# Dealing out a generator's pieces anew: layer 2's early keys and values in a four-layer kernel on one core

## The chip, the cores and the metric

The kernel runs as one program on one core of one Trainium2 chip. The metric is the device time of one execution in microseconds, less is better. Before the change it is 2393.62 us, the median of three runs (2391.97 to 2395.31). One more execution, taken with the hardware profiler, is the one that the rows in this document come from.

## The reference: what is computed

A stack of four layers works on tokens x of shape (4, 256, 256) and on a context of shape (4, 1601, 256), all float32. Each layer is a cross step followed by a feed-forward network, both added to x:

- Layer 0: softmax attention of the tokens over the masked context, then a mixture of 32 experts (96 inner channels), of which each token takes 8.
- Layer 1: a summary of the context by a decayed scan, added through layer norms, then 8 experts with 2 for each token and a shared expert.
- Layer 2: attention with 16 heads of 128 channels and 4 key/value heads, over the 1601 keys and values of the context and causally over the 256 tokens of the batch. Keys are normed (root mean square). Then 4 experts, 1 for each token.
- Layer 3: attention with 32 heads of 8 channels over the context, then a feed-forward network with quantised weights.

What matters for this change is one part of layer 2. Its context keys and values depend on the context and on weights alone, not on x:

```
k_ctx = rms_norm(ctx @ wk_ctx) * k_norm_w      # per batch and key/value head: 1601 x 128
v_ctx = ctx @ wv_ctx                            # per batch and key/value head: 1601 x 128
```

So they can be made at any time before layer 2's first scores.

## The kernel before

The kernel is written as a sequence of stages, layer by layer. The order of instructions on each engine is mostly that of the program text, rearranged by a scheduler in the framework where instructions are not pinned; semaphores are derived from the tiles' uses.

**The early pieces.** `l2_early` (from L1263) is a generator that makes the context keys and values of layer 2 for 16 units (4 batches by 4 key/value heads). It yields after each of 176 pieces, 11 for a unit:

- Seven product pieces. Six hold four matmuls (L1307) from `ctxT` and the unit's weights into one tile of the accumulator memory, 128 rows each for two chunks of the context. The last holds two matmuls with 96 rows. A matmul appears as two records in the profile. ScalarE (ACT) copies the keys to `kr_early` (L1314) and the values to `va_early` (L1315), and the SP queue writes the values to DRAM (L1316, `vd`). After some pieces ACT squares the keys into `sq_early`, a tile with one buffer (L1325), and VectorE (DVE) sums them (L1326).
- The norm of the unit: a square root on ACT and a reciprocal on DVE (L125, L126), and four multiplications (L1332) by the engine in `self.scaler`. That is GpSimd (POOL), but DVE inside `l0_add` and at the end of `l1_ffn`.
- Four turn pieces, for the unit before: 4, 4, 4 and 1 transposes (L1341), each piece copied by ACT into `kT_early` (L1343, 4 buffers) and written by SP (L1344, `kd`).

**Where pieces are advanced.** `self.fill(n)` (L174) advances the generator by n pieces; what it issues stands in the program at that place. The counts are constants at the top of the file:

- three pieces at the start of layer 0's attention;
- `F0[4]` = 6 behind layer 0's router logits, `F0[5]` = 8 within `slots`, which counts the tokens of each expert, `F0[6]` = 4 at each of four parts of the matmuls that build `src`, the list of tokens sorted by expert (L512), and `F0[7]` = 4 after the gathers by `src` are issued on POOL (L522);
- `G0` = 9 at each of nine steps of `l0_add`, which gathers the experts' results and adds them to x, 81 in all;
- `F1` = 1, 2, 2, 3 in `normed` (L187) ahead of layer 1's FFN, one count for each batch, between the layer norm `xn` (L160) and its transposes `tp_ln` (L191);
- `G1`, 30 in sum, at the end of layer 1's FFN, between the adds of its results to x (L981);
- `LN2` = 2, `Q2` = 2 and `C2` = 6 in layer 2's first `prep`, behind the norm of the first batch (transposes `tp_ln`, L1425), and behind the first queries;
- what is left is drained ahead of the first scores:

```
            for n, _ in enumerate(prep(0, w, ready)):
                self.fill(Q2 if n == 0 else C2 if n == 3 else 0)
            for _ in self.early:
                pass
            self.es2.close()
```

Before the change ten pieces are left for this drain (the three last products of unit 15, the turns of units 14 and 15 in part). `prep` makes the tokens' own queries and keys of a unit: `tpq` (projection of the queries), `tpkv` (keys and values), the steps `qo` and `ko` on DVE and POOL (L1482 to L1516), the transposes `tpqT` (L1526) and `tpk` (L1531). Then the scores `s` start.

**Layer 0's expert loop.** In `l0_ffn` the sorted tokens form 95 tiles. `brought(n)` transposes a gathered tile `f0xr` (L561, `f0tpx`), `through(n)` does the first matmuls (`f0gu`), `turned(n)` transposes the inner values (`f0tph`), `down(n)` does the second ones (`f0y`). `brought` runs two tiles ahead:

```
            brought(0)
            brought(1)
            for s in range(NS + 2):
                if s < NS:
                    hs[s] = through(s)
```

Within this loop there are no early pieces.

Of the kernel before, what the change touches and what calls it, by code (L numbers as in the profile page):

```python
# [44 lines left out]
CT2 = NM - 1  # L45


F0 = [0, 0, 0, 0, 6, 8, 4, 4]
G0 = 9
REGS = 4  # L50
F1 = [1, 2, 2, 3]
G1 = [7, 4, 4, 3, 2, 2, 2, 2, 2, 2, 0]
LN2, Q2, C2 = 2, 2, 6
FIRST3 = [7, 1, 3]
# [43 lines left out]
class Kernel:  # L98
# [311 lines left out]
    def l0_ffn(self, one):  # L410
# [17 lines left out]
        with ExitStack() as es:  # L428
# [21 lines left out]
            nc.gpsimd.tensor_scalar(start, tok[:, 0:1], float(P), None, ALU.mult)  # L450
            xT = self.normed(ps, F0[:B], xd)
            next(loads)
# [4 lines left out]
            for t in range(8):  # L457
                for k in range(2):
                    self.mm(lg[:, t, :], xT[t // 4][:, k, (t % 4) * P : (t % 4 + 1) * P], wr[:, k, :], k == 0, k == 1)
            self.fill(F0[B])  # L460
            next(loads)
# [10 lines left out]
            nc.vector.tensor_single_scalar(oh, oh, GONE, ALU.is_equal)  # L472
            cum, end = self.slots(rt, "f0", E0, oh, products(), low, keep, lambda: self.fill(F0[B + 1]))
            next(loads)
# [18 lines left out]
            for part in range(4):  # L493
                ones = []
                for t in range(2 * part, 2 * part + 2):
# [9 lines left out]
                    ones.append((t, rows, cols))  # L505
                self.fill(F0[B + 2])
                next(loads, None)
# [26 lines left out]
            nc.vector.tensor_copy(ei, er[:1, :NS])  # L534
            self.fill(F0[B + 3])

# [21 lines left out]
            def brought(n):  # L558
                tp = ps.tile([P, 2, P], F32, name="f0tpx", tag="tp")
                for k in range(2):  # L560
                    nc.tensor.transpose(tp[:, k, :], xr[n][:, k * P : (k + 1) * P], self.ident)  # L561
                t = two.tile([P, 2, P], F32, name="f0xsT", bufs=4)
                nc.scalar.copy(t, tp)
                xsT.append(t)
                if n % REGS == 0:
                    expert.extend(self.registers(ei[:, n : min(n + REGS, NS)], E0))

            def through(n):
                gu = products()[:, : 2 * I0]
                for k in range(2):  # L570
                    self.mm(gu, xsT[n][:, k, :], w13[:, bass.ds(expert[n], 1), k, :], k == 0, k == 1)
                h = two.tile([P, I0], F32, name="f0h", bufs=3)
                nc.scalar.activation(h, gu[:, :I0], AF.Silu)
                nc.vector.tensor_tensor(h, h, gu[:, I0:], ALU.mult)
                return h

            def turned(h):
                tp = ps.tile([P, P], F32, name="f0tph", tag="tpf")
                nc.tensor.transpose(tp[:I0], h, self.ident)
                hT = two.tile([I0, P], F32, name="f0hT", bufs=3)  # L580
                nc.scalar.copy(hT, tp[:I0])
                return hT

            def down(n, hT):
                y = ps_y.tile([P, 512], F32, name="f0y", tag="y")[:, :D]
                self.mm(y, hT, w2[:, bass.ds(expert[n], 1), :], True, True)
                ys = two.tile([P, D], F32, name="f0ys", bufs=6)
                nc.vector.tensor_copy(ys, y)
                nc.sync.dma_start(yd[n * P : (n + 1) * P, :], ys)

            hs, hTs = {}, {}
            brought(0)
            brought(1)
            for s in range(NS + 2):
                if s < NS:
                    hs[s] = through(s)
                    if s + 2 < NS:
                        brought(s + 2)
                if 0 <= s - 1 < NS:
                    hTs[s - 1] = turned(hs.pop(s - 1))  # L600
                if s >= 2:
                    down(s - 2, hTs.pop(s - 2))
                if s >= 20 and s % 4 == 0:
                    next(gated, None)
# [166 lines left out]
    def l1_ffn(self, weights):  # L771
# [11 lines left out]
        with ExitStack() as es:  # L783
# [14 lines left out]
            low, keep, lane, tok = self.low, self.keep[:, :E1], self.lane, self.tok  # L798
            xT = self.normed(ps, F1[:B], xd, rt)

# [1687 lines left out]
```

## Time and profile before

| | us |
|---|---|
| median of three runs | 2393.62 |
| profiled execution, device time | 2387.69 |
| its span, first to last instruction | 2386.0 |
| around the span | 1.69 |
| TensorE (PE) busy | 2255.6 |
| DVE busy | 1473.2 |
| ACT busy | 1272.4 |
| POOL busy | 948.7 |

The mean granted clock of PE is 0.973 of full speed. Where rows of the profile are shown, a timeline row has the start in the span, the duration, the engine, the line, the operation with its tiles, the count, and in brackets the idle time before it with what released it. A row of a window has its limits and length, then the busy time of PE, of weight loads, DVE, ACT and POOL with the number of instructions, then PE's clock, the share of the DMA engines and their rate in GB/s. A row of waits has the total, the times and the longest.

### The profile page before, as it was taken

How to read it: one execution, taken by the hardware profiler on the slowest of the kernel's cores; microseconds unless marked ns; L12 is line 12 of the kernel's file. 1: busy time of each engine (PE TensorE's matmuls, PEld its weight loads, DVE VectorE, ACT ScalarE, POOL GpSimd, SP SyncE). 2: the span in 40 equal slices, each digit the busy share in tenths (PEclk: the TensorE clock that was granted, in tenths of full speed). 3: DMA queues.
4: the chain of work that ended last, by engine and by line, in shares of the span. 5: the costliest groups of instructions: out<-in, count | busy, mean ns of one | idle time of the engine just before them, and what ended most of it. 6: DMA issues, size and time to landing. Idle time of an engine off the chain costs nothing.

```text
span 2386.0 us, 42230 instructions
## 1 busy us (share of the span) xinstructions
PE 2255.6 (95%) x14335; PEld 1382.2 (58%) x14335; DVE 1473.2 (62%) x3553; ACT 1272.4 (53%) x2877; POOL 948.7 (40%) x1707
## 2 busy tenths in 40 slices
PE   8989997889989999999999999999899889999996
PEld 5677875777745555555555655555665533444332
DVE  5453532773457777777777777777334574758344
ACT  3334443552474555555555555553232577888994
POOL 1014655503335544555554555554121253334220
PEclk9989998989999999999999999999899999999998
DMA  7165575652550111111111111100534353434320
GB/s 267 41 201 161 172 156 157 197 185 65 167 179 32 43 51 47 47 51 51 51 52 51 51 51 50 44 10 10 205 124 117 114 156 103 109 94 103 83 64 19
DMA packets 156078, 234.47 MB, mean 98 GB/s; under 512 B 33929, under 2 KB 122761, under 8 KB 154666
## 3 DMA queue, kind: packets, MB, share of 16 engines
q1 hardware_dynamic: 138998, 190.07, 25.0%
q0 software_dynamic: 11280, 31.60, 5.4%
q10 hardware_dynamic: 5588, 10.09, 1.4%
q8 instruction: 117, 1.92, 0.3%
q14 instruction: 95, 0.78, 0.1%
HBM read 169.94 MB, written 61.74 MB: 97 GB/s over the span
## 4 chain that ended last, share of the span: by engine, by line
PE 78%; DVE 7%; issue 5%; DMA 4%; ACT 2%; POOL 2%; SPq 1%; ACTq 0%; POOLq 0%; DVEq 0%
PE o L117 17%; PE s L117 17%; PE o L77 6%; PE b L77 3%; PE f2gu L117 3%; PE s L77 3%; PE f1gu L117 2%; PE fill L1307 2%; PE f0gu L117 2%; PE acc L117 2%; PE tpq L117 2%; PE av L117 2%; PE f0y L117 2%; PE f2y L117 1%; PE f1y L117 1%
## 5 line engine op out<-in xcount | busy, mean ns | idle before, releaser
L1572 ACT ACTIVATE p<-s,nmsm 128x448 f32<-128x448 f32 (+2 forms) x512 | 324.7, 639 | 369.6 <-DVE nmsm L1567 317.4
L117 PE MATMUL o<-pT,va 128*128 128x256 f32 (+2 forms) x1920 | 431.7, 377 | 3.3 <-DVE pT L1613 2.9
L117 PE MATMUL s<-kT,qT 128*32 128x448 f32 (+2 forms) x4096 | 424.2, 550 | 4.2 <-ACT p L1572 4.2
L77 ACT ACTIVATE e<-s 128x1024 f32<-128x1024 f32 (+1 forms) x416 | 392.4, 1041 | 57.4 <-PE s L77 56.3
L117 PEld LDWEIGHTS o<-pT,va 128*128 128x128 f32 (+1 forms) x1920 | 344.7, 190 | 127.9 <-issue 75.4
L1607 POOL TENSOR_SCALAR p<-p,rm 128x448 f32<-128x448 f32 (+2 forms) x512 | 320.7, 649 | 6.3
L1567 DVE TENSOR_REDUCE nmsm<-s 128x1 f32<-128x448 f32 (+4 forms) x384 | 293.2, 783 | 4.4
L1613 DVE STREAM_TRANSPOSE pT<-p 128x448 f32<-128x448 f32 (+4 forms) x384 | 278.1, 778 | 11.1 <-POOL p L1607 11.1
L117 PEld LDWEIGHTS s<-kT,qT 128*32 128x32 f32 x4096 | 121.7, 109 | 250.2 <-issue 213.9
L77 PE MATMUL o<-e,va 128*32 128x512 f32 x1656 | 246.9, 614 | 12.3 <-DVE os L77 12.2
L1600 POOL TENSOR_TENSOR rm<-em,tot 32x8 f32<-32x8 f32 x256 | 50.3, 197 | 335.6 <-DVE tot L1597 303.3
L1564 DVE TENSOR_TENSOR s<-s,mask 128x64 f32<-128x64 f32 (+4 forms) x384 | 92.5, 260 | 128.5 <-PE s L117 82.4
L77 PEld LDWEIGHTS s<-qb,kb 32*128 32x128 f32 (+1 forms) x1664 | 65.5, 180 | 182.3 <-issue 143.7
L1307 PE MATMUL fill<-wkc_early,ctxT 128*128 128x256 f32 (+1 forms) x444 | 110.5, 401 | 8.9 <-ACT va_early L1315 6.7
L522 POOL DMA_INDIRECT f0xr<-f0xd,f0src x95 | 91.3, 961 | 66.5 <-PE f0y L117 25.5
L77 PE MATMUL s<-qb,kb 32*128 32x256 f32 (+1 forms) x1664 | 111.5, 331 | 3.1 <-ACT e L77 1.8
L77 POOL CAST kb<-kf 128x384 fp32r<-128x384 f32 (+1 forms) x126 | 65.5, 549 | 96.4 <-PE s L77 61.8
L1307 PEld LDWEIGHTS fill<-wkc_early,ctxT 128*128 128x128 f32 (+1 forms) x444 | 87.0, 200 | 25.3 <-ACT va_early L1315 7.8
L1572 ACT ACTIVATION_READ_ACCUMULATOR p<-s,nmsm 128x1 f32 x512 | 100.5, 196 | 0.0
L1326 DVE TENSOR_REDUCE ss_early<-sq_early 128x4 f32<-128x512 f32 x64 | 37.1, 580 | 82.8 <-ACT sq_early L1325 72.0
L630 POOL DMA_INDIRECT f0yt<-f0yd,f0slot x64 | 63.1, 987 | 60.7 <-DVE x L622 29.8
L117 PE MATMUL f2gu<-f2wgu,f2xsT 128*128 x176 | 85.1, 608 | 0.6 <-ACT f2xsT L114 0.3
(579 smaller groups left out, 3689.2 us busy)
## 6 DMA issues: line engine op xcount, KB each, us to landing
kf<-kd SPq DMA_DIRECT2D x384, 48.0 KB
vd<-va_early SPq DMA_DIRECT2D x96, 128.0 KB
kd<-kT_early SPq DMA_DIRECT2D x48, 256.0 KB
kT<-kd SPq DMA_DIRECT2D x16, 768.0 KB
va<-vd SPq DMA_DIRECT2D x16, 768.0 KB
kd<-kt SPq DMA_DIRECT2D x96, 128.0 KB
f0yd<-f0ys SPq DMA_DIRECT2D x95, 128.0 KB
ctxT<-in_ctxT SPq DMA_DIRECT2D x5, 1664.0 KB
```

The costliest lines, as they stand in the source:

```text
L77: ins = f(*a, **kw)
L117: self.ordered(self.nc.tensor.matmul(out, lhsT, rhs, start=start, stop=stop, **kw))
L522: nc.gpsimd.indirect_dma_start(out=t, out_offset=None, in_=xd[:, :], in_offset=bass.IndirectOffsetOnAxis(ap=src[:, n : n + 1], axis=0),)
L630: nc.gpsimd.indirect_dma_start(out=yt, out_offset=None, in_=yd[:, :], in_offset=bass.IndirectOffsetOnAxis(ap=slot[:, t, r : r + 1], axis=0),)
L1307: ins = nc.tensor.matmul(tp[:rows, t, :], ctxT[u // NKV2][:, k, c0 : c0 + rows], w[u % NKV2][:, k, :], start=k == 0, stop=k == 1,)
L1326: nc.vector.tensor_reduce(ss[:, m0:m1], sq[:, : m1 - m0, :], AX.X, ALU.add)
L1564: nc.vector.tensor_tensor(sv, sv, mask[:, e0:e1, : nt - CT, :].rearrange("p n t i -> p n (t i)"), ALU.add)
L1567: nc.vector.tensor_reduce(ms[:, 0, e0:e1], s[:, n0:n1, : nt * 32], AX.X, ALU.max, negate=True)
L1572: nc.scalar.activation(p[:, n, : nt * 32], s[:, n, : nt * 32], AF.Exp, bias=ms[:, 0, e : e + 1], accum_out=ms[:, 1, e : e + 1],)
L1600: nc.gpsimd.tensor_tensor(r[32 * a : 32 * a + 32], e[:, a], tot, ALU.mult)
L1607: nc.gpsimd.tensor_scalar(p[:, n, : nt * 32], p[:, n, : nt * 32], r[:, e : e + 1], 1.0, ALU.mult, ALU.mult)
L1613: self.pin(nc.vector.transpose(pT[:, 2 * c + n0 : 2 * c + n1, :nt, :].rearrange("p n t i -> p n (t i)"), p[:, n0:n1, : nt * 32],))
```

## The change

Four places get other counts. One piece more comes behind layer 0's router logits; one piece each is advanced between `brought(0)` and `brought(1)` and after the first `through`; one piece more comes in the first batch of `normed` ahead of layer 1's FFN. Since the pieces come in a fixed order, every later place advances other pieces than before: `l0_add` those numbered 40 to 120 (before: 37 to 117), the end of layer 1's FFN 130 to 159 (126 to 155), layer 2's `prep` 160 to 169 (156 to 165). The drain ahead of the scores is left with six pieces in place of ten.

```diff
-F0 = [0, 0, 0, 0, 6, 8, 4, 4]
+F0 = [0, 0, 0, 0, 7, 8, 4, 4]
 G0 = 9
 REGS = 4
-F1 = [1, 2, 2, 3]
+F1 = [2, 2, 2, 3]
...
             brought(0)
+            self.fill(1)
             brought(1)
             for s in range(NS + 2):
                 if s < NS:
                     hs[s] = through(s)
+                    if s == 0:
+                        self.fill(1)
                     if s + 2 < NS:
                         brought(s + 2)
```

## The prediction

> **What bounds the kernel now.** I read the page first: the busy line and the chain of waits.
>
> ```profile
> PE 2255.6 (95%) x14335; PEld 1382.2 (58%) x14335; DVE 1473.2 (62%) x3553; ACT 1272.4 (53%) x2877; POOL 948.7 (40%) x1707
> PE 78%; DVE 7%; issue 5%; DMA 4%; ACT 2%; POOL 2%; SPq 1%; ACTq 0%; POOLq 0%; DVEq 0%
> ```
>
> TensorE (PE) is busy for 95% of the span and carries 78% of the chain. The change adds and removes no matmul: it moves early pieces. So it can pay only where PE idles, or runs at a reduced clock, and a piece moved there no longer stands on PE elsewhere. The second view is therefore the table of windows, for the stages that the four edits touch (columns: PE, weight loads, DVE, ACT, POOL, then clock, DMA share, GB/s).
>
> ```profile
> 137.00:204.00 67.00, 60.94 (x270) 49.82 (x270) 33.45 (x107) 26.13 (x67) 10.95 (x13) 0.87 0.58 186
> 204.00:216.00 12.00, 7.54 (x39) 5.76 (x38) 1.79 (x6) 6.06 (x17) 8.83 (x9) 0.94 0.73 234
> 512.00:526.00 14.00, 13.22 (x47) 10.49 (x47) 4.61 (x18) 6.54 (x11) 3.40 (x4) 0.53 0.80 257
> 619.00:654.00 35.00, 33.89 (x172) 29.46 (x170) 19.03 (x52) 20.30 (x56) 14.41 (x15) 1.00 0.72 217
> 654.00:691.00 37.00, 28.85 (x127) 20.68 (x125) 18.42 (x49) 24.77 (x61) 15.47 (x19) 0.93 0.70 240
> 691.00:720.00 29.00, 24.78 (x186) 8.17 (x186) 21.79 (x50) 21.02 (x54) 10.94 (x25) 0.92 0.23 80
> ```
>
> Layer 0's routing (137 to 204) idles PE for 6 us of 67, its first gathers (204 to 216) for 4.5 of 12, layer 2's opening (654 to 691) for 8 of 37. Behind layer 1's first norm (512 to 526) PE is full but at clock 0.53. The end of layer 1's FFN (619 to 654) has only 1 us to spare. The waits of the gathers, of layer 1's norm, and of the opening, in three answers:
>
> ```profile
> PE f0tpx L561 <- DMA f0xr<-f0xd,f0src: 3.4, 2, 1.9
> PE f0gu L117 <- DMA vd<-va_early: 1.0, 1, 1.0
> ```
> ```profile
> 510.36 1.77 PE L191 MATMUL tp_ln<-ident,xn 128*128 128x128 f32 x8 [2.00 <-DVE xn L160]
> ```
> ```profile
> 653.59 0.60 PE L1425 MATMUL tp_ln<-ident,xn 128*128 128x128 f32 x4
> 658.87 2.02 PE L1307 MATMUL fill<-wkc_early,ctxT 128*96 128x256 f32 x4 [4.67 <-ACT va_early L1315]
> ...
> 671.87 1.89 PE L117 MATMUL tpkv<-wks,xT 128*128 128x256 f32 x8
> 673.60 5.34 PE L1307 MATMUL fill<-wkc_early,ctxT 128*128 128x256 f32 x24
> 679.89 0.66 PE L1526 MATMUL tpqT<-ident,qo 128*128 128x128 f32 x4 [0.96 <-POOL qo L1516]
> ...
> 683.94 1.98 PE L117 MATMUL tpq<-wq,xT 128*128 128x512 f32 x4
> 687.81 0.66 PE L1341 MATMUL fill<-ident,kr_early 128*128 128x128 f32 x4 [1.88 <-POOL kr_early L1332]
> 688.81 2.33 PE L1341 MATMUL fill<-ident,kr_early 128*128 128x128 f32 x9 [0.34 <-POOL kr_early L1332]
> 691.07 1.53 PE L117 MATMUL s<-kT,qT 128*32 128x416 f32 x8
> ```
> ```profile
> 684.69 1.28 ACT L125 ACT_TABLE_LOAD   x1
> ```
> ```profile
> 686.71 3.40 POOL L1332 TENSOR_TENSOR kr_early<-kr_early,ss_early 128x512 f32<-128x512 f32 x4 [5.88 <-DVE ss_early L126]
> ```
>
> This is the stage to read. The first unit's own keys and queries are turned by tpqT at 679.89 and by tpk, which ends at 683.2; the copy of tpk to kT ends at 683.9. The scores start 7.2 us later, because the rest of the early pieces is drained first: the last unit's norm waits for a table load, then POOL multiplies for 3.40 us, then come its transposes.
>
> **The change part by part**, against the profiled execution of 2387.69 us (span 2386.0 and 1.69 around it), which lies 5.93 below the median of the three runs, 2393.62. The median gets the same difference.
>
> *One piece more at layer 0's router (F0[4] 7 for 6).* In the instruction order, one product piece of four matmuls (eight records, 1.73 us at full clock in the chain's row, 2.0 at 0.87) stands on PE before the counts, and equally many matmuls stand before the first gather's transposes in both kernels. What can move is the gather list: later by 0 to 2.0. PE has gaps of 2.58, 1.21 and 1.80 us around the counts, so I take +0.6. Its ACT copies (two of 0.38) and its write on SP come earlier with it; ACT is busy for 26 of 67 us.
>
> *Two pieces among the first gathers.* They hold nine transposes with the one that shifts in (12 took 1.96 us, so 1.5), beside 4.5 us in which PE waits for DMA: nothing. Without that cover they cost 1.5. Three ACT copies of 0.69 stand ahead of the tile's own (ACT is busy for 6 of 12), and three writes of 256, 256 and 64 KB join gathers at a DMA share of 0.73. Bounds 0 to +1.5, taken 0.
>
> *One piece more at layer 1's first norm (F1[0] 2 for 1).* Up to tp_ln, PE gets four product matmuls more (+1.73), and four transposes between the later tp_ln go (-0.6). From 484 to 511 PE idles 5.3 us, 2.00 of them at the wait for xn, which DVE ends and PE's load doesn't touch: 0, with +1.7 as the upper bound. The lower bound is the half-clock stretch: if it follows from the idling, filling that saves up to 14 x (1 - 0.53) = 6.6 us.
>
> The Trainium skill ("TensorE: Matmul & The Clock Gate", HAM oscillation) puts the fall to half clock behind idle gaps of over about 3.4 us; by it, this piece would remove no slow stretch here, since the gap was 2.00.
>
> *End of layer 1's FFN.* PE's load there is equal (33.2 us against 33.3). The norm of unit 14 now falls on DVE (four multiplications in 2.08 and a reciprocal of 0.24) among the adds to x, for which layer 2's first norm waits; before, POOL did it at 663.17. DVE is busy for 19 of 35 us, so I take about half, +1.3: tp_ln ends at 655.5 and not 654.2. Bounds 0 to +2.3.
>
> *Layer 2's opening.* The stall of 4.67 us comes from ACT, whose copies queue behind squares with a single buffer, which DVE frees late, behind the adds. The stalled piece is now a transpose piece, and I take 1 us for the stall (0 to 5.3). From 656.5 PE's list up to tpkv is, start to start in the rows of before: a transpose 0.1, 12 products 5.2, tpq 1.72, 7 products 3.02, tpq 1.80, 7 products 3.0, tpkv 1.73: 16.6, so tpkv ends at 673.1. Before, it ended at 673.6. The first unit's chain after it (ko 0.97 and 0.73, qo 2.04 on POOL, tpqT, tpk, copies) is unchanged, but the last unit's norm now comes before it on POOL: ready some 1.7 us after the last product at 671.4, so POOL is held from 673.2 to 676.6, ko ends at 678.3 and qo at 680.4, where before qo ended at 680.84. So tpk's copy ends near 683.7 as before, and the scores start there and not at 691.07: -7.4. Left for later is unit 1's first tpq, which stood ahead of the scores. Bounds: a stall of 0 gives -8.4; one of 5.3 gives -3.1; POOL's 3.40 in full gives -4.0. The two other table loads fall after or out of this stretch; the one on the chain is worth 1.28 and is in the 7.4.
>
> The Trainium skill ("ScalarE: Activation LUTs", What ACT_TABLE_LOAD costs) puts a switch at 2.66 us with its drain. Here ACT's next instruction started 1.30 us after the load began, so the row goes; by the page I would have 1.4 us more for each load taken away.
>
> *Given back.* The moved tpq brings 1.98 us of PE, 0.59 of ACT, 2.05 of DVE and 1.27 of POOL into the first unit's scores, where DVE is busy for 21.8 of 29 us and PE idles 4.2: +1.2, bounds 0 to 2.05.
>
> Sum: 0.6 + 0 + 0 - 7.4 (the +1.3 is in it) + 1.2 = -5.6: 2382.1 for the profiled execution, 2388.0 for the median.
>
> **The rivals.** *A, the slow clock goes too.* The piece at layer 1's norm, or its other timing, ends the stretch at 0.53: 6.6 us, of which I count 6.0, so -11.6 and 2382.0. For it: the idle stands directly before the fall. Against it: 2.01 us of idle at 491.91 was followed by no fall.
>
> *B, the stall stays.* ACT's queue still blocks PE for 5.3 us in the opening: -3.1 + 0.6 + 1.2 = -1.3, so 2392.3. For it: the squares keep their one buffer. Against it: the transposes at the front use buffers that ACT empties earlier.
>
> *C, slower: the opening idles PE into half clock.* With 24 product records gone from behind tpkv, PE has 21 transposes (3.4 us) between 673.1 and tpqT at 680.4, so it idles for 4 us, where it idled 0.96. At layer 1's norm 2.00 us was enough for a stretch at 0.53. Price: 14 us of it cost 6.6, 20 us cost 9.4; with 9.4 and the gather list late by the full 2.0 (+1.4 on the 0.6) the sum is -5.6 + 9.4 + 1.4 = +5.2, so 2398.8. It decides if the granted clock is near 0.5 for over 12 us from 680 on. Against it: waits of 1.88 and 0.34 us just before 691 leave 691 to 720 at 0.92.
>
> By the page on the clock gate just named, an idle of 4 us in the opening is over the window, and this rule speaks against the change; one window of some 3.4 us at half clock would cost about 1.7 us, by estimate.
>
> **How the numbers follow.** The forecast has 0.48, its own range -8.5 to -3.0 (2385.1 to 2390.6); 0.2% or 4.8 us, about what a measurement of this kernel can tell, cuts off 0.09 of it as "same". A has 0.13, B 0.14, C 0.25. Faster: 0.39 + 0.13 = 0.52; same: 0.09 + 0.14 = 0.23; slower: 0.25. The range runs from A with a stall of 0 and the rest of the 6.6 (-13.2, 2380.4, rounded to 2380) to just above C's centre (2400), which leaves out some 0.15.
>
> **What would show it.** Right: scores that start about 7 us sooner after layer 2's tp_ln than 36.9 us, no wait on POOL's kr_early ahead of them, the first f0tpx less than 1 us later, equal spans from there to tp_ln of layer 1. Wrong: a gap of over 3 us for ACT's va_early or kT_early after layer 2's tp_ln (B); a clock near 0.5 behind 680 (C); a clock near 1 in the 14 us after layer 1's first tp_ln (A); or a loop of layer 0, untouched by the edits, that changes its length by more than 3 us.

## The result, and the profile after

The changed kernel takes 2400.31 us (median of 22 runs, 2395.95 to 2404.85), the kernel before 2394.76 (22 runs, 2389.08 to 2403.33). The ratio is 1.0023, 95% interval 1.0017 to 1.0030: 5.5 us slower, where 5.6 us faster was forecast.

The profiled execution took 2404.85 us, its span 2403.1. It lies 4.5 us above its median, and that of before 7.1 us below the median of the 22. So of the 17 us between the two profiles only a third is the change; a difference counts below only where other profiles repeat it. From the page of the changed kernel, busy line and chain:

```profile
PE 2266.2 (94%) x14322; PEld 1390.5 (58%) x14335; DVE 1476.9 (61%) x3557; ACT 1269.6 (53%) x2875; POOL 948.0 (39%) x1703
PE 79%; DVE 8%; issue 4%; POOL 3%; DMA 3%; ACT 2%; SPq 1%; ACTq 0%; POOLq 0%; DVEq 0%; another core or an unknown queue 0%
```

PE is busy for 10.6 us more with the same matmuls: they ran at a lower clock (0.967 in the mean, 0.973 before). DVE and POOL each have one hundredth more of the chain. The windows of the changed kernel, moved to where the stages now lie (layer 0's gathers, `l0_add`, behind layer 1's `tp_ln`, layer 2's opening), and ahead of them `l0_add` in the kernel before:

```profile
365.00:510.40 145.40, 116.29 (x539) 96.24 (x537) 88.23 (x217) 68.53 (x196) 63.15 (x64) 0.89 0.59 186
```
```profile
206.00:218.00 12.00, 7.16 (x31) 6.08 (x32) 1.43 (x5) 5.92 (x14) 9.23 (x10) 0.72 0.91 293
367.00:521.00 154.00, 121.72 (x548) 98.93 (x548) 90.50 (x219) 69.96 (x201) 67.85 (x68) 0.88 0.55 176
521.00:538.50 17.50, 16.62 (x54) 12.49 (x55) 6.34 (x22) 6.25 (x9) 0.00 (x0) 0.51 0.72 229
667.00:700.00 33.00, 26.54 (x109) 20.46 (x109) 16.30 (x41) 19.09 (x48) 9.73 (x12) 0.83 0.67 230
```

`l0_add` is 8.6 us longer, and the clock in the opening is 0.83 where it was 0.93. The waits at layer 1's norm and in the opening (timeline rows of PE, then one of POOL):

```profile
521.10 2.04 PE L191 MATMUL tp_ln<-ident,xn 128*128 128x128 f32 x8 [2.98 <-DVE xn L160]
...
666.99 0.78 PE L1428 MATMUL tp_ln<-ident,xn 128*128 128x128 f32 x4 [2.71 <-issue]
669.44 0.48 PE L1344 MATMUL fill<-ident,kr_early 128*128 128x128 f32 x1 [1.67 <-ACT kT_early L1346]
669.71 8.01 PE L1310 MATMUL fill<-wkc_early,ctxT 128*128 128x256 f32 x24
...
687.03 1.89 PE L117 MATMUL tpkv<-wks,xT 128*128 128x256 f32 x8
...
691.87 0.33 PE L1344 MATMUL fill<-ident,kr_early 128*128 128x128 f32 x1 [1.63 <-ACT kT_early L1346]
...
695.84 1.12 PE L1529 MATMUL tpqT<-ident,qo 128*128 128x128 f32 x4 [1.79 <-POOL qo L1519]
...
700.23 2.33 PE L117 MATMUL s<-kT,qT 128*32 128x416 f32 x11
```
```profile
689.75 3.55 POOL L1335 TENSOR_TENSOR kr_early<-kr_early,ss_early 128x512 f32<-128x512 f32 x4 [1.61 <-DVE ss_early L126]
```

The opening has the forecast order: transpose, 24 product records, tpq, 14, tpq, 14, tpkv, then POOL's norm ahead of ko and qo, and no wait on `kr_early` just ahead of the scores. But the 24 records took 8.01 us, not 5.2: the clock was halved from 668.3 to 675.1. Layer 1's `tp_ln` waits 2.98 us for DVE, where it waited 2.00.

Stage by stage, from the starts of timeline rows, one profile for each column. The last four columns are from the experiments, on other chips. In `l0_add` on the first chip, waits of PE that the profile names "issue" (waits for nothing that it shows) fill about 24 us. The chip on which the kernel before takes 2389 us has them too (20 to 23 us in four profiles); on those at about 2345 us they are 1.4 us or less.

| stage, us | before | changed | changed, 2389 chip | before, 2345 chip | changed, 2345 chip | changed with first step 6 |
|---|---|---|---|---|---|---|
| to the last f0y | 365.0 | 367.2 | 366.5 | 362.1 | 361.0 | 362.8 |
| `l0_add`, to tp_ln of layer 1 | 145.4 | 153.9 | 149.9 | 110.2 | 113.7 | 109.3 |
| to the first f1tpx | 49.8 | 51.1 | 51.1 | 50.1 | 49.9 | 44.9 |
| to tp_ln of layer 2 | 93.4 | 94.8 | 95.0 | 91.9 | 93.0 | 93.6 |
| opening, to the scores | 37.5 | 33.2 | 30.8 | 37.5 | 33.1 | 31.3 |
| scores to the end | 1694.9 | 1702.9 | 1694.3 | 1693.5 | 1692.9 | 1689.6 |

The 8 us behind the scores are in no other profile of the changed kernel. What repeats: the opening gains 4.2 to 6.7, `l0_add` loses 3.5 to 8.6, the rest little. For the 2389 chip there is no profile of the kernel before, so its column is held against that of the first chip.

### The profile page after: what moved, and what is told of

Its sections match the earlier page's. It is cut to its first block, busy times and chain, and to the rows that moved or that the text cites. A ratio compares the mean times of both kernels' runs of the same rounds, so it can differ in the third digit from the quotient of the medians.

```text
span 2403.1 us, 42213 instructions
## 1 busy us (share of the span) xinstructions
PE 2266.2 (94%) x14322; PEld 1390.5 (58%) x14335; DVE 1476.9 (61%) x3557; ACT 1269.6 (53%) x2875; POOL 948.0 (39%) x1703
## 4 chain that ended last, share of the span: by engine, by line
PE 79%; DVE 8%; issue 4%; POOL 3%; DMA 3%; ACT 2%; SPq 1%; ACTq 0%; POOLq 0%; DVEq 0%; another core or an unknown queue 0%
PE o L117 17%; PE s L117 16%; PE o L77 7%; PE b L77 3%; PE fill L1310 3%; PE f2gu L117 3%; PE s L77 3%; PE f1gu L117 2%; PE f0gu L117 2%; PE acc L117 2%; PE tpq L117 2%; PE av L117 2%; PE f0y L117 2%; PE f2y L117 1%; PE f1y L117 1%
## 5 line engine op out<-in xcount | busy, mean ns | idle before, releaser
L77 PE MATMUL o<-e,va 128*32 128x512 f32 x1656 | 249.5, 620 | 12.5 <-DVE os L77 10.6
L77 PE MATMUL s<-qb,kb 32*128 32x256 f32 (+1 forms) x1664 | 111.7, 332 | 4.0 <-ACT e L77 1.8
```

Of the source, the lines that this page charges most:

```text
L77: ins = f(*a, **kw)
```

## The experiments

Each time is compared with that of the kernel before on the same chip, which took 2342 to 2346 us on four of the chips and 2389 us on one. Theory 1: the pieces shift the order of DVE's queue in `l0_add` (the "phase": which pieces' reduces stand ahead of which add). Theory 2: chance in the profiles. Theory 3: the start of layer 0's loop. Theory 4 came after the first four runs: without the issue stalls, what counts is the stretch at half clock behind layer 1's tp_ln, and the opening.

**The shift alone.** `G0` becomes a list in the kernel before, nothing else is changed:

```diff
-G0 = 9
+G0 = [12, 9, 9, 9, 9, 9, 9, 9, 6]
-            self.fill(G0)
+            self.fill(G0[t])
```

> The kernel before, with one thing else: the nine steps of l0_add advance 12, 9, 9, 9, 9, 9, 9, 9, 6 pieces in place of nine times 9. Every stage holds the pieces that it had; within l0_add each add to x stands behind three pieces more, as in the changed kernel. Theory 1 (the phase: DVE works in order, the first add of l0_add waits behind the reduces of three product pieces more, and the gathers that wait for free rows follow): the first add comes 3 to 6 us later after the last f0y than in the kernel before (42.9 us there, 45.9 in the changed kernel), layer 1's tp_ln 4 to 8 us later (145.4 before, 153.9 in the changed kernel), the time 4 to 8 us above the kernel before. Theory 2 (the 8.5 us there are chance: where the windows at half clock and the issue stalls fell in the one profile): within 2 us of the kernel before. Theory 3 (the later start, by the piece at the router and the pieces between the gathers): within 2 us, since nothing of that is in this kernel.

Measured 1.0015 (1.0005 to 1.0025), 3.5 us. The first add came 26.7 us after the last f0y, where the kernel before took 22.3 on another chip without the stalls; tp_ln 112.5 against 110.2. Theory 1 holds for the first add and in sign, below its range in the rest. Theories 2 and 3 had it within 2 us, which the interval (1.2 to 5.9 us) doesn't exclude.

**The mirror image:**

```diff
-G0 = 9
+G0 = [6, 9, 9, 9, 9, 9, 9, 9, 12]
```

> The kernel before with steps of 6, 9, 9, 9, 9, 9, 9, 9, 12 pieces in l0_add: the mirror image of the run with 12 to 6. Theory 1: the first add of l0_add comes 2 to 4 us sooner, the time 2 to 5 us below the kernel before. Theory 4: the stage as long as before within 1.5 us; the time within 2 us, unless the stretch at half clock behind layer 1's tp_ln changes.

0.9970 (0.9958 to 0.9982), 7 us faster. The first add came at 18.3, tp_ln at 108.8: 1.5 us of the 7. The greater part stood behind tp_ln: PE had no wait for xn, no half clock followed, and the stretch to f1tpx took 44.7 us in place of 50.1, the exception that theory 4 named. The first adds, from the DVE timelines of the kernel before (its last f0y at 362.1), of 12 to 6 (358.0) and of 6 to 12 (359.0):

```profile
384.44 3.10 DVE L622 SCALAR_TENSOR_TENSOR x<-f0yt,f0gate,x 128x256 f32<-128x256 f32 x6
```
```profile
383.22 0.69 DVE L1326 TENSOR_REDUCE ss_early<-sq_early 128x4 f32<-128x512 f32 x1 [2.77 <-ACT sq_early L1325]
384.34 0.28 DVE L1326 TENSOR_REDUCE ss_early<-sq_early 128x1 f32<-128x128 f32 x1 [0.43 <-ACT sq_early L1325]
384.75 1.00 DVE L622 SCALAR_TENSOR_TENSOR x<-f0yt,f0gate,x 128x256 f32<-128x256 f32 x2
```
```profile
377.27 0.47 DVE L622 SCALAR_TENSOR_TENSOR x<-f0yt,f0gate,x 128x256 f32<-128x256 f32 x1
```

With steps of 12 to 6, DVE waits 2.77 and 0.43 us for the squares of pieces that now stand ahead, and the first add follows them.

**The single parts of the change.** Router, `F0[4]` 7 for 6; the two fills among the gathers; `F1[0]` 2 for 1; each alone in the kernel before.

```diff
-F0 = [0, 0, 0, 0, 6, 8, 4, 4]
+F0 = [0, 0, 0, 0, 7, 8, 4, 4]
```

> The kernel before with only the piece more behind layer 0's router logits: each later place advances pieces one further, the drain is left with nine. Theory 1 (phase, one piece of three): 0 to 3 us above the kernel before, the first add of l0_add 1 to 2 us later after the last f0y. Theory 3 (the gather list comes later by the piece): 2 us above it, all of them before the first f0tpx, and l0_add as long as before. Theory 2 (chance): 0 to 2 us below.

0.9966 (0.9955 to 0.9977), 7 us faster: above the gain of up to 2 us that theory 2 had, and against the other two. From the token counts to the last f0y it took 220.3 us, where the two kernels without the piece on its chip took 216.9 and 218.2, so it is some 2 us late, as theory 3 says; the gain is behind: 45.6 us from tp_ln to f1tpx, and 31.3 from layer 2's tp_ln to the scores.

```diff
             brought(0)
+            self.fill(1)
             brought(1)
...
                     hs[s] = through(s)
+                    if s == 0:
+                        self.fill(1)
```

> The kernel before with only the two pieces among the first gathers (38 and 39 as the order stands, here 37 and 38): l0_add begins two pieces later, the drain is left with eight. Theory 1 (phase, here two pieces of three): 2 to 5 us above the kernel before. Theory 2 (chance): 1 to 3 us below it, since the drain is shorter by two. Theory 3 (the start): the pieces delay the first tiles by 1 to 3 us, which the shorter drain about makes up: within 2 us.

0.9988 (0.9974 to 1.0001): within the range of theories 2 and 3, below that of theory 1. Up to the last f0y it loses nothing. But in the stage theory 1 shows here too: the first add came at 24.9 us, tp_ln at 111.7 behind a wait of 1.94, and the stretch to f1tpx took 52.5, with 20.5 at half clock. That is some 4 us more than in the kernel before; the opening, at 33.8 us, gives about as much back.

```diff
-F1 = [1, 2, 2, 3]
+F1 = [2, 2, 2, 3]
```

> The kernel before with only F1[0] = 2: one product piece more ahead of layer 1's first tp_ln, all before it unchanged, the drain left with nine. Theory 1: no phase is moved in l0_add, 0 to 2 us below the kernel before. Theory 4: the time follows the stretch at half clock behind tp_ln: 2 to 6 us below the kernel before if the stretch is shorter than 7 us, within 2 us if it stays at 14 or more.

0.9962 (0.9948 to 0.9976), 9 us faster and more than either theory had, and 0.9960 (0.9945 to 0.9975) in the repeat:

> The kernel before with only F1[0] = 2, again. If its 0.38% were the shorter stall behind layer 2's first tp_ln (5 us) and the shorter stretch at half clock (1.5 us in the profile): 5 to 9 us below the kernel before on a chip of either kind. If they were of the chip: within 3 us.

The opening is 31.3 us. At layer 1's tp_ln DVE's chain is as long as in the kernel before (9.88 us from the last add), but PE has one piece more and waits 0.28 us, not 2.00; 10.2 and 3.4 us at half clock follow in the two profiles, not 13.7. This PE timeline shows why one piece is enough: the last product of unit 14 is now done before the stage, its transposes stand around tp_ln, and the first tpq starts 3.5 us after tp_ln began, not 8.7.

```profile
610.77 0.67 PE L1425 MATMUL tp_ln<-ident,xn 128*128 128x128 f32 x3 [1.12 <-DVE xn L1417]
611.27 1.04 PE L1341 MATMUL fill<-ident,kr_early 128*128 128x128 f32 x8
...
614.25 1.88 PE L117 MATMUL tpq<-wq,xT 128*128 128x512 f32 x4
```

So the three parts are each no loss here, two of them a clear gain. All three together are the changed kernel:

> The changed kernel, unchanged, beside the kernel before on the same chip. Theory 1: 4 to 7 us above it, as on record (ratio 1.0023), the loss in l0_add. Theory 4: if the chip shows no issue stalls in l0_add, 0 to 4 us below the kernel before, since the run with phase restored was 1.5 us below and that stage was the same within 1 us; if it shows them, about 5 us above.

0.9992 (0.9983 to 1.0000), 2 us faster, in the range of theory 4. A second and a third time:

> The changed kernel again. On a chip without the issue stalls in l0_add (before at 2344 us): 0 to 3 us below the kernel before, as in the first run there. On one with them (before at 2394 us): 4 to 7 us above, and then the other three of this call show on it whether l0_add's order (the run with a first step of 6) or the opening (the run with F1[0] = 5) makes the loss.

> The changed kernel a third time. On a chip without issue stalls in l0_add 0 to 3 us below the kernel before, as twice measured; on one with them 4 to 7 us above it.

0.9996 (0.9985 to 1.0007), and on the chip with issue stalls 1.0006 (0.9997 to 1.0016): 1.4 us above, by the interval between 0.7 below and 3.8 above, so the 4 to 7 us above did not come there. The 5.5 us of the result were measured on the first chip alone. The kernel before for comparison, one run of 2347.11 us:

> The kernel before, unchanged, for a profile beside those of the first four runs, which took 2344 us for it where the shown time was 2394. Theory 1 (the phase in l0_add decides): from the last f0y to layer 1's tp_ln 108 to 112 us, less than the 112.5 of the run with steps 12 to 6. Theory 4 (that stage is no longer where the change acts, once the issue stalls of some 25 us in it are missing; what differs is the stretch at half clock behind layer 1's tp_ln and layer 2's opening): the stage as long as in the other runs within 1.5 us, from tp_ln to the first f1tpx about 50 us with some 14 us of them at half clock (45.6 with 3.4 in the run with the router's piece alone), from layer 2's tp_ln to the scores about 37.

Theory 4 holds for the stretch to f1tpx (50.1, 13.7 of it at half clock) and the opening (37.5); `l0_add` took 110.2, which is within theory 1's range too.

**Putting the order back in the changed kernel.** First with the three pieces at the last step, then without them:

```diff
-G0 = 9
+G0 = [6, 9, 9, 9, 9, 9, 9, 9, 12]
```

> The changed kernel, but the nine steps of l0_add advance 6, 9, 9, 9, 9, 9, 9, 9, 12 pieces: up to its last step each add stands behind the same pieces as in the kernel before, and the three pieces more come after the adds. All else as changed, the drain of six pieces too. Theory 1 (the phase in l0_add): the first add 41 to 43 us after the last f0y, 5 to 8 us taken off the changed kernel, so 0 to 3 us below the kernel before. Theory 2 (chance in one profile): like the changed kernel, 5 us above the kernel before. Theory 3 (the later start): like the changed kernel too, 4 to 6 us above the kernel before.

0.9993 (0.9983 to 1.0003), within theory 1's range for the time, but the same as the changed kernel: the first add is back (21.4), the last is not (101.3 against 100.4 before and 102.6 changed), and tp_ln still waits 2.79 us, with 17.1 us at half clock around it.

```diff
-G0 = 9
+G0 = [6, 9, 9, 9, 9, 9, 9, 9, 9]
```

> The changed kernel with a first step of 6 pieces in l0_add, the others 9: l0_add advances pieces 40 to 117, so all adds stand behind the pieces that they stood behind before, and the drain is left with nine. What stays of the change: the piece at the router, the two pieces among the gathers (now pure relief for l0_add) and the piece at layer 1's norm. Theory 1 (phase and the three products more in l0_add cost, the other pieces not): l0_add 107 to 110 us, the opening 31 to 32 as with F1[0] = 2 alone, 8 to 12 us below the kernel before. Theory 3 (the pieces at the router and the gathers cost 2 us or more in the start of the loop): 4 to 8 us below it.

0.9950 (0.9933 to 0.9967), 12 us faster, on the chip on which the changed kernel was at 0.9996. Repeated, and again on a chip without the stalls:

> The changed kernel with a first step of 6 pieces in l0_add, again. If the order in l0_add makes the loss everywhere: 6 to 12 us below the kernel before on a chip of either kind, no half clock behind layer 1's first tp_ln, a wait of less than 1 us ahead of it. If the issue stalls decide where they occur (before at 2389 to 2394): within 4 us of the kernel before there.

0.9966 (0.9953 to 0.9979). What differs between the two is seen in three views: the changed kernel first (2345 us chip), the one with a first step of 6 second. PE at layer 1's tp_ln:

```profile
474.75 2.08 PE L191 MATMUL tp_ln<-ident,xn 128*128 128x128 f32 x8 [3.12 <-DVE xn L160]
476.76 1.88 PE L117 MATMUL f1gu<-r,xnT 128*128 128x8 f32 x8
```
```profile
472.06 1.52 PE L191 MATMUL tp_ln<-ident,xn 128*128 128x128 f32 x8 [0.28 <-DVE xn L160]
473.71 1.06 PE L117 MATMUL f1gu<-r,xnT 128*128 128x8 f32 x8
```

The 15 us behind it, by the windows:

```profile
474.70:489.70 15.00, 14.17 (x50) 11.02 (x50) 6.28 (x21) 5.66 (x8) 0.00 (x0) 0.51 0.78 252
```
```profile
472.10:487.10 15.00, 13.32 (x77) 10.19 (x78) 8.38 (x46) 10.35 (x19) 3.39 (x4) 1.00 0.90 284
```

50 records of matmuls against 77 in the same time. And DVE ahead of it, with the POOL row that matters:

```profile
465.39 1.94 DVE L160 TENSOR_SCALAR y<-x,ln_mv,ln_rs 128x256 f32<-128x256 f32 x2
467.37 1.41 DVE L1268 TENSOR_TENSOR y<-y,sm 128x512 f32<-128x512 f32 x1
```
```profile
465.10 3.94 POOL L1335 TENSOR_TENSOR kr_early<-kr_early,ss_early 128x512 f32<-128x512 f32 x4 [13.66 <-DVE ss_early L126]
```
```profile
464.37 0.74 DVE L160 TENSOR_SCALAR y<-x,ln_mv,ln_rs 128x256 f32<-128x256 f32 x2
465.14 0.69 DVE L1268 TENSOR_TENSOR y<-y,sm 128x512 f32<-128x512 f32 x1
```

Against the kernel before, whose last add came at 100.4 us, the changed kernel's `l0_add` is 3.5 us longer: 2.2 up to the last add and 1.3 from there to tp_ln. Against the one with a first step of 6, the chain that ends at xn is longer for two reasons: the last add starts at 102.6 us after the last f0y and not at 99.4, and the steps of y take 3.35 us and not 1.43, while POOL multiplies the norm of unit 11 (at 479.69 in the other kernel, behind tp_ln). PE has meanwhile run out of pieces and waits 3.12 us, and the half clock follows.

**Telling these two apart** worked in part. In the first of three edits of the changed kernel POOL's norm stayed where it was, 9.7 us ahead of tp_ln:

```diff
-F1 = [2, 2, 2, 3]
+F1 = [2, 1, 2, 4]
```

> The changed kernel with F1 = 2, 1, 2, 4 in place of 2, 2, 2, 3: the norm of unit 11 comes a batch later in the program, all else in layer 0 and layer 2 as changed. If the norm on POOL beside DVE's layer norm is the cause: it runs behind tp_ln, the two steps y take 0.41 us each and not 0.9 to 1.12, tp_ln comes 1.9 us sooner, the stretch at half clock is shorter, 4 to 8 us below the kernel before. If the phase or the last step's products are: within 2 us of it, like the changed kernel.

1.0014 (1.0003 to 1.0026), on the chip with stalls: inconclusive, since the edit did not move what it was to move.

```diff
-G0 = 9
+G0 = [9, 9, 9, 9, 9, 9, 9, 9, 6]
```

> The changed kernel with the last of the nine steps of l0_add at 6 pieces: adds stand behind the same reduces as in the changed kernel until the last step, but pieces 118 to 120 follow in layer 1's norm; the drain is left with nine. If the last step's products are the cause: like the run with a first step of 6, tp_ln 109 to 110 us after the last f0y, no more than 7 us at half clock behind it, 9 to 13 us below the kernel before. If the phase is: the first add at 25.7 us and tp_ln at 112 to 114 us, a wait of 2 us or more ahead of it, 0 to 5 us below.

1.0019 (1.0009 to 1.0029) on that chip: the loss is there without the last step's products. With the phase of the changed kernel the wait was even 4.26 us, and 18 us at half clock followed, as its second case says, though that case's gain did not come.

```profile
514.23 2.08 PE L191 MATMUL tp_ln<-ident,xn 128*128 128x128 f32 x8 [4.26 <-DVE xn L160]
```

POOL's norm started only during the last step of y here, and the three steps took 1.48 us in sum, so that slowing isn't needed for the wait; the same holds for the steps of 12 to 6, with a wait of 4.00. In both PE also has three pieces fewer in the last step. In the run with steps of 6 to 12 in the changed kernel it is the other way round: the first adds are back, the three pieces stand in the last step, y is slowed, and tp_ln waits 2.79. So the phase is enough for a wait longer than the 2.00 of before, and so are the last step's pieces with the slowed y; how the changed kernel's 3.12 divides between them is not shown.

```diff
-G0 = 9
+G0 = [3, 9, 9, 9, 9, 9, 9, 9, 12]
```

> The changed kernel with steps of 3, 9, 9, 9, 9, 9, 9, 9, 12 in l0_add (pieces 40 to 117, each add behind three pieces fewer than in the kernel before). If the phase helps by itself: 1 to 3 us below the run with steps of 6 and then 9, so 12 to 15 us below the kernel before. If only tp_ln's wait and the clock matter: as that run, 10 to 13 us below.

0.9991 (0.9981 to 1.0001) on that chip: no wait and no half clock behind tp_ln, 44.9 us to f1tpx, but `l0_add` took 150.2 us there, with 41 us of it at half clock around the stalls. The forecast of 10 us and more fell. The first add came at 23.2 us, where the changed kernel had 46.4 on this chip, and the stage was as long as its 149.9: with the stalls, no run shows that the order of the adds sets the stage's length.

**The other half, the opening**, in the kernel before, so that layer 0 is untouched and the drain has six pieces:

```diff
-F1 = [1, 2, 2, 3]
+F1 = [5, 2, 2, 3]
```

> The kernel before with F1[0] = 5 in place of 1: layer 0 as before, and from layer 1's FFN on every place advances the pieces that it advances in the changed kernel (130 to 159 at its end, 160 to 169 in prep, a drain of six). Opening theory (a drain of six is worse than one of nine, because 26 product matmuls and not 16 stand ahead of tpkv, and PE idles enough around them to lose its clock): tp_ln to scores 31 to 34 us with some 10 us at half clock, 3 to 5 us less than before; the three products more ahead of layer 1's tp_ln cost 2 to 4 us; in all 0 to 3 us below the kernel before. If the opening's loss in the changed kernel came from the start (other transfers in flight): 28 to 30 us, and 4 to 7 us below.

0.9966 (0.9955 to 0.9978), 8 us faster; tp_ln of layer 2 to the scores 30.1 us, PE idle for 4.0 us ahead of tpqT. That lies below the first alternative's 31 to 34, with 6 us at half clock in place of 10, and the time is nearer to the second. So six pieces for the drain are no loss by themselves. The order in the opening is that of the changed kernel, but the 24 product records ran at full clock:

```profile
619.88 5.35 PE L1307 MATMUL fill<-wkc_early,ctxT 128*128 128x256 f32 x24
```

In the four profiles of the changed kernel they took 6.69 to 8.23 us. Beside this run, the changed kernel on a 2345 us chip is 2.2 us longer in `l0_add` and 3.0 in the opening.

**A version that beats both.** The kernel before with two of the edits above:

```diff
-G0 = 9
+G0 = [6, 9, 9, 9, 9, 9, 9, 9, 12]
-F1 = [1, 2, 2, 3]
+F1 = [2, 2, 2, 3]
```

> The kernel before with F1[0] = 2 and with steps of 6, 9, 9, 9, 9, 9, 9, 9, 12 pieces in l0_add: the two single changes that were 0.4% and 0.3% below it, together. If the gains are of different places (the opening's stall, tp_ln to queries 8.7 us before and 3.5 with F1[0] = 2; the adds sooner in l0_add, its end 1.5 us sooner, and the half clock behind layer 1's tp_ln gone), they add up but for the half clock that both lower: 9 to 13 us below the kernel before. If both only won by where the half clock fell: 5 to 9 us below, as each alone.

0.9956 (0.9939 to 0.9973): 10 us faster, in the first range, and less than the 16 that the two alone would add up to. With the changed kernel's other pieces and a first step of 6 it is 0.9950 and 0.9966; the three can't be told apart by these intervals. All these gains were measured on chips without the issue stalls.

## Why the prediction was wrong

- **`l0_add`, for which the sum has no term: the step that failed.** I asked of each place what PE's load there would be, and had equal spans from the first f0tpx to tp_ln of layer 1 among the signs of being right. The nine steps of `l0_add` hold as many pieces as before, but numbers 40 to 120 in place of 37 to 117. DVE works through its queue in order (the rows of the steps of 12 to 6), so pieces moved ahead of an add put their reduces, and the PE and ACT work under these, ahead of that add. From the first f0tpx to tp_ln I had +0; measured were 302.5 us before and 314.8 after on the first chip, 264.0 and 267.4 on a 2345 us chip. In `l0_add` alone it is 8.6 and 3.5 us. The 3.5 take most of the opening's gain. On the chips without the stalls the runs that move nothing but the order (12 to 6, 6 to 12) and the changed kernel with a first step of 6 show the link. For the 8.6 us, and so for the sign of the result, they don't: no experiment met a chip on which the changed kernel loses 5 us.
- **Layer 1's norm, 0.** That DVE ends the wait for xn "and PE's load doesn't touch" it is right for the moment at which it ends: with `F1[0]` = 2 alone tp_ln came at 110.0 us and not at 110.2. It left out that DVE's own chain would be longer, and that the wait's length counts for the clock. The wait grew from 2.00 to between 2.97 and 3.12 us although PE had a piece more, and the stretch at half clock behind tp_ln's start was 14.6 to 17.1 us in all profiles of the changed kernel, 13.7 before, 0 with a first step of 6. My bounds of +1.7 and -6.6 had the right place for the clock and only its good side.
- **Router's piece, +0.6.** On the 2345 us chips the last f0y comes 222.0 us after the counts in six profiles with it (220.2 to 225.5), 219.5 in eight without it (216.9 to 222.5): +2.4 on average, a little above my upper bound of 2.0, with a spread as large in either group.
- **Pieces among the gathers, 0.** Nothing speaks against it: from the first f0tpx to the last f0y 151.5 us in the one profile with them alone, 151.8 to 154.3 without.
- **End of layer 1's FFN, +1.3.** Right: 93.0 against 91.9, and 94.8 against 93.4.
- **Opening, -7.4 with that 1.3.** The order, the release (a stall of 0.7 to 1.7 us where I took 1) and POOL's norm came as worked out. From the start of tp_ln to the scores I had 28.8 us; 33.2, 33.1 and 31.7 were measured, 30.8 on the 2389 chip. The missing term is the clock: 2.8 us on the first 24 records, which stand behind the waits at tp_ln (2.71 and 1.67 us in the first profile). I priced these waits as time alone. With F1 = 5, 2, 2, 3 the same order without that half clock took 30.1.
- **Given back, +1.2.** Not to be told apart: from the scores to the end 1692.9 against 1693.5.
- **Rival A** was on the table as a gain (the slow stretch gone, 6.6 us). It is what the runs with `F1[0]` = 2, a first step of 6, or the router's piece alone collect in part or in full (44.9 to 48.5 us to f1tpx against 50.1); the changed kernel doesn't. What I held against it, 2.01 us of idle at 491.91 without a fall, is answered below.
- **Rival C**, at 2398.8, lies near the measured 2400.31, but by luck. Its half clock behind the 4 us of idle did come, 6.8 to 10.2 us long in the four profiles and not over 12; the first half clock of the opening lies elsewhere, on the 24 records, and C has nothing of `l0_add`.

The sum by the 2345 us chip, in the order of the table, is -1.1 + 3.5 - 0.2 + 1.1 - 4.4 - 0.6 = -1.7, that of the spans, and near the measured ratios of 0.9992 and 0.9996. On the first chip `l0_add` costs more, and there the kernel is slower. What stays open is why: whether the 8.6 us are the rule there (the 2389 chip has the stalls too, and a ratio of 1.0006), and what the issue stalls are. PE, ACT and DVE stand or do little while POOL issues gathers, on some chips and not on others. I have no run that takes them away.

## What to carry to other kernels

Work that is dealt into gaps has consequences on every in-order queue that it crosses: ask of each moved piece which later instruction on DVE or POOL now stands behind it, not only whether PE has room. A wait of PE is worth more than its length when it costs the clock, so pieces are best placed where they end just before the operand that PE waits for arrives; here the stretch to f1tpx was 5 us shorter (50.1 to 44.9) where no half clock followed. And try the parts alone: two of them gained 7 to 9 us each, and all three together at most 2. That they spoil each other by the shift that they add up to fits the runs on chips without stalls; no run has two of the three parts.

## What the runs showed of the hardware

The trace's record of the granted clock changes only at steps of 3.41 us. I compared, in the 20 profiles, how busy PE was in each such window at full clock (from layer 0's routing to shortly before the end) with the clock of the next one. After a window that was less than 40% busy the next was at half clock in all of some 130 cases; between 40% and 50% in about 6 of 7; between 50% and 60% in about 3 of 10; above 60% in 18 of nearly 12,000. Back to full clock it came only after a window that was over 70% busy. So a wait of 2 us is enough when it falls within one window, and may cost nothing when it straddles two. Of the waits of PE of 1.9 to 3.0 us at full clock, all 33 that lay within one window were followed by half clock, and 5 of 22 that lay across two with less than 1.4 us in either; of the 65 between, 46. In the kernel before, the wait of 2.00 us ahead of 510.36 lies within one window (508.06 to 511.48); that of 2.01 ahead of 491.91 is cut by a window's start at 491.00. In 11 profiles layer 1's tp_ln waited 1.9 us or more and 13.7 to 20.5 us at half clock followed, in 9 it waited 1.4 us or less and 0 to 10.2 followed. Where the windows lie differs from execution to execution; how much of the 14 us between the lowest and the highest run of the kernel before comes from it was not measured. The Trainium skill ("TensorE: Matmul & The Clock Gate", "HAM oscillation — how this bites in real kernels") asks for no idle gaps over about 3.4 us; the window length agrees with these runs, the size of the gap doesn't.

DVE's steps of y became 2.3 times as long in sum while POOL multiplied (1.94 against 0.74 us, 1.41 against 0.69). The Trainium skill ("SBUF — State Buffer", "SBUF: two separate sides") speaks of a port pair that DVE and GpSimd share, by an exclusive lock; the runs show the slowing, not the lock.
